# Four casts moved from ScalarE to VectorE, and a table load moved ahead of a copy, at the passage from attention to feed-forward

## The chip, the cores and the metric

The kernel runs on one core of one Trainium2 chip. The metric is the device time of one execution in microseconds (us). Engines are named as in the profile: PE is TensorE (matrix multiply; PEld are its weight loads, which overlap), ACT is ScalarE, DVE is VectorE, POOL is GpSimd, SP is SyncE, whose queue (SPq) issues nearly all transfers.

## The reference

One transformer layer on x of shape (4, 512, 512): cross-attention with 32 heads of 16 channels and rotary positions, added to x, and then a feed-forward part with ternary weights, added again. Cut to the parts that the change touches:

```python
x = x + xattn(layernorm(x), ctx, pos, ctx_pos, Wq, Wkv, Wout, bout)   # softmax attention
x = x + ffn(layernorm(x), w_fc, w_proj)

def ffn(x, w_fc, w_proj):
    h = bitlinear(x, w_fc)          # (4, 512, 512) -> (4, 512, 2048)
    h = gelu(h)                     # exact gelu
    return bitlinear(h, w_proj)     # back to 512

def bitlinear(x, w):                # x_hat is layernorm(x), rounded in the forward value
    return einsum('bsd,od->bso', x_hat, sign(round(w / mean|w|)) * mean|w|)
```

## The kernel before

**Attention.** For each of the 4 batches the 32 heads are taken in 8 groups of 4, so there are 32 groups, and each group has 8 units. A unit's logits are made twice: once with queries on the partitions (`logits`, for the row maxima, which VectorE reduces in `maxima`) and once with keys on the partitions, less the maxima (`exponentials`), of which ScalarE takes the exponential into a tile `es` (L570). Two such tiles are then multiplied with the values in `weigh` (L580), which gathers the group's `av` in one PSUM bank. `attended` ends a group: ScalarE copies `av` to the SBUF tile `avs` (L597), SP stores it (L598), and for every second group the sums are read back (L609), inverted on VectorE (L613), stored (L614), broadcast (L618) and multiplied into `aT` on GpSimd (L619). `aT` is the attended tile that the output projection reads.

**Passage.** The feed-forward part of batch 0 needs x of batch 0, normalised (`prepare`, L736, on VectorE), transposed on PE into PSUM (`first_T`, L749), and split into two parts: a high part `dTh` that is the value rounded to the matrix format fp32r (L753, a copy with a cast) and a low part `dTl`, the value less the high part (L754, VectorE). Four tiles of 128 tokens go through it. They are done during the last two groups of attention, as "chores" that `first_chore` puts into a queue. The chore's transposes come in one burst of units, the split is put off to the next one. All four tiles share one PSUM bank (`tp_d`), so the transposes of a tile wait for both readers of the tile before.

**Order.** The order on PE, DVE, ACT, SP and POOL is that in which the program text issues the work (a manual schedule). After the loop over bursts, the text weighs what is left, calls `attended` for the last group, runs everything that was put off (the split of the fourth tile among it), and then runs one gelu of a single column, so that the gelu table is loaded on ScalarE (L1006). A table load is an instruction of ScalarE's own queue.

**Feed-forward.** For each batch and each of 16 blocks of 128 hidden channels, `first` multiplies 8 times (L1039: four blocks of channels, high and low part) into a PSUM tile `hp` of which there are two, ScalarE takes gelu (L1047) into `h`; `split` makes the high part `hh` (L1053) and the square on ScalarE and the low part `hl` and the sums on VectorE; `second` multiplies them with the second matrix (L1077). The SBUF of the attention's tiles is given to the feed-forward's. The tiles of batches 1 to 3 go through the same `first_T`, but inside the feed-forward's loop, where `first_T(...)()` transposes and splits at once. At hidden blocks 6 to 9 of batch 0 the output projection of batch 3 is done (L1158).

Of the kernel before, what the change touches and what calls it, by code (L numbers as in the profile page):

```python
# [9 lines left out]
F32 = mybir.dt.float32  # L10
F32R = mybir.dt.float32r
AF = mybir.ActivationFunctionType
# [3 lines left out]
P = 128  # L16
# [15 lines left out]
def xattn_ffn(  # L32
# [13 lines left out]
    nc = tc.nc  # L46
# [5 lines left out]
    KD, KC, KF = D // P, C // P, F // P  # L52
# [18 lines left out]
    small = ctx.enter_context(tc.tile_pool(name="small", bufs=4))  # L71
# [84 lines left out]
    ones = const.tile([P, P], F32, name="ones")  # L156
# [136 lines left out]
    def put_off(k, f, end=0):  # L293
        later[end].setdefault(k, []).append(f)

    def run(k, end=0):
        for f in later[end].pop(k, []):
            f()

    def bank(name, spare=False):  # L300
        if spare:
            return ps_v.tile([P, S], F32, name=name, tag="v")
        if prologue[0]:
            return ps_s.tile([P, 2, S], F32, name=name, tag="s")[:, 0, :]
        return ps_t.tile([P, S], F32, name=name, tag="t")
# [267 lines left out]
    def weigh(i, c, es, av):  # L573

        b, g = divmod(i, NG)
        for r in range(2):
            for h in range(2):
                j = 2 * r + h
                v0 = (g * HG + j) * VS
                nc.tensor.matmul(  # L580
                    av[j * HP : (j + 1) * HP, :],
                    va[b % 2][:, c, v0 : v0 + HP],
                    es[r][:, h, :],
                    start=c == 0,
                    stop=c == NT - 1,
                )
# [3 lines left out]
    def attended(i, av, k):  # L590

        b, g = divmod(i, NG)
        n = g // 2
        avs = apool.tile([P, S], F32, name=f"avs{i}", tag="avs", bufs=1)
        nc.scalar.copy(avs, av)  # L597
        nc.sync.dma_start(av_d[b][g * P : (g + 1) * P, :], avs)  # L598
        if g == 0:
            aT[b] = big.tile([P, KD, S], F32, name=f"aT{b}", tag="aT", bufs=2)  # L600
        if g % 2 == 0:
            return
        rows = av_d[b][n * 2 * P : (n + 1) * 2 * P, :].rearrange("(h r) s -> h r s", r=HP)
        W = 2 * HG * S // P
        den = small.tile([P, W], F32, name=f"den{i}", tag="den", bufs=2)
        rec = rden_d[b][n * 2 * HG : (n + 1) * 2 * HG, :]

        def fetch():
            nc.sync.dma_start(den, rows[:, HD, :].rearrange("h (q w) -> h q w", w=W))  # L609
            nc.sync.dma_start(aT[b][:, n, :], rows[:, 0:HD, :])  # L610

        def invert():
            nc.vector.reciprocal(den, den)  # L613
            nc.sync.dma_start(rec.rearrange("h (q w) -> (h q) w", w=W), den)  # L614

        def spread():
            rb = big.tile([P, S], F32, name=f"rb{i}", tag="rb")
            nc.sync.dma_start(rb, rec.unsqueeze(1).to_broadcast([2 * HG, HD, S]))  # L618
            nc.gpsimd.tensor_tensor(aT[b][:, n, :], aT[b][:, n, :], rb, ALU.mult)  # L619

        put_off(k + 2, fetch, 1)
        put_off(k + 6, invert, 1)
        put_off(k + 7, spread, 1)
# [114 lines left out]
        )  # L738
        return d

    def first_T(i, d, tp):
        b, t = divmod(i, NT)
        if t == 0:
            dT[b] = (
                big.tile([P, KD, S], F32R, name=f"dTh{b}", tag="aT", bufs=2),
                big.tile([P, KD, S], F32R, name=f"dTl{b}", tag=f"va{b % 2}"),
            )
        for k in range(KD):
            nc.tensor.transpose(tp[:, k, :], d[:, k * P : (k + 1) * P], ident)  # L749

        def split():
            high, low = (x[:, :, t * P : (t + 1) * P] for x in dT[b])
            nc.scalar.copy(high, tp)  # L753
            nc.vector.tensor_tensor(low, tp, high.bitcast(F32), ALU.subtract)  # L754

        return split

    def first_chore(t, ready):
        split = []

        def step(p, _):
            split.append(first_T(t, first_d.pop(t), p.rearrange("p (k n) -> p k n", k=KD)))

        return Chore(f"tp_d{t}", 1, step, lambda p, k: put_off(k + 1, split[0]), 0.7, ready)

# [7 lines left out]
    p = bank("warm")  # L773
# [122 lines left out]
    av, es, first_d = {}, {}, {}  # L896
# [3 lines left out]
    for k, burst in enumerate(bursts):  # L900
        run(k)
        for kind, s in burst:
            i, u = divmod(s, NU)
# [48 lines left out]
        while due and due[0][0] <= k:  # L952
            _, j, c, e = due.pop(0)
# [43 lines left out]
    assert not queue and not urgent and open_chore is None, (len(queue), len(urgent))  # L997
    for _, j, c, e in due:
        weigh(j, c, e, av[j])
    left = sorted(later[0].keys() | later[1].keys())  # L1000
    attended(n_groups - 1, av.pop(n_groups - 1), left[-1])
    for k in left:
        run(k)
        run(k, 1)

    nc.scalar.activation(small.tile([P, 1], F32, name="gelu_1", tag="gelu_1"), ones[:, 0:1], AF.Gelu)  # L1006
    left = sorted(later[1])
    run(left[0], 1)
    order.__exit__(None, None, None)
# [21 lines left out]
    def xbank(name):  # L1031
        return ps_x.tile([P, KD, P], F32, name=name, tag="x")
# [96 lines left out]
    with tc.manual_schedule(engines=ordered):  # L1129
        gam4 = small.tile([P, NT], F32, name="gam4", tag="gam4")  # L1130
        nc.gpsimd.tensor_scalar(gam4, ones[:, 0:NT], gam_pr[:, 0:1], None, ALU.mult)
        steps = [(b, f) for b in range(B) for f in range(KF)]
        todo = list(steps)
        after = {}
        ds = {}
        hold = 0

        def behind(n, f):
            after.setdefault(n, []).append(f)


        for n, s in enumerate(left[1:]):
            behind(2 + n, lambda s=s: run(s, 1))

        for n in range(len(steps) + 4):
            on = n < len(steps)
            if on:
                b, f = steps[n]
                first(b, f)
                split(b, f)  # L1150
                if f == KF - 1 and b + 1 < B:
                    behind(n + 1, lambda b=b: totals(b))

            if on and b == 0 and 6 <= f < 6 + NT:
                t = f - 6
                p = xbank(f"op{B - 1}_{t}").rearrange("p k n -> p (k n)")
                for k in range(KD):
                    nc.tensor.matmul(  # L1158
                        p,
                        aT[B - 1][:, k, t * P : (t + 1) * P],  # L1160
                        wout_sb[:, k, :],
                        start=k == 0,
                        stop=k == KD - 1,
                    )
                i = (B - 1) * NT + t
                nc.vector.tensor_tensor(x_sb[:, i, :], p, x_sb[:, i, :], ALU.add)
            if on and b + 1 < B:
                at = (10, 11, 13, 14) if b == 0 else (6, 9, 12, 14)
                for t in range(NT):
                    i = (b + 1) * NT + t  # L1170
                    if f == at[t] - 4:
                        stats(i)
                    elif f == at[t] - 2:
                        ds[i] = prepare(i, fpool, "d")
                    elif f == at[t]:
                        first_T(i, ds.pop(i), xbank(f"tp_d{i}"))()
            if n == 3:
                nc.vector.tensor_copy(ones_r, ones)
            if n == 7:
                column_sums()  # L1180
            count = 0
            while todo and count < 2 and n >= hold:
                sb, sf = todo[0]
                m = sb * KF + sf
                if on and n - m < 2:
                    break
                if sb == B - 1 and sf >= KF - 2:
                    break
                todo.pop(0)
                count += 1  # L1190
                for t in range(NT):
                    second(sb, sf, t)
                if sf == KF - 1:
                    hold = n + 3
                    for t in range(NT):
                        behind(n, lambda b=sb, t=t: centered(b, t))
                        behind(n + 1 + t, lambda b=sb, t=t: finish(b, t))
                    break
            for x in after.pop(n, []):
                x()  # L1200
            if not on and len(todo) == 2:
                break
        for n in sorted(after):
            for x in after[n]:
                x()

        for t in range(NT):
            for sb, sf in todo:
                second(sb, sf, t)
            if t == 0:  # L1210
                totals(B - 1)
            centered(B - 1, t)
            if t > 0:
                finish(B - 1, t - 1)
        finish(B - 1, NT - 1)
# [50 lines left out]
```

## Time and profile before

| what | value |
|---|---|
| median of 3 runs | 845.94 us (845.82 to 846.93) |
| profiled execution | 843.32 us, span 841.5 us |
| PE busy | 813.5 us, 97% of the span |
| DVE busy | 616.3 us, 73% |
| ACT busy | 456.6 us, 54% |
| POOL busy | 299.9 us, 36% |
| clock granted to PE | 0.998 of full speed |
| cast of one tile on ACT (L753) | 16 of them, 578 ns in the mean |
| low part of one tile on DVE (L754) | 16 of them, 688 ns in the mean |
| table load on ACT (L1006) | 1283 ns |
| first matmul of the feed-forward | at 571.05 us |

The span is the time from the first to the last instruction that the profile shows; the execution's own time is a little longer. A row of the profile names the line of the program, the engine, the operation, what it writes and reads (tile names without their numbers), how often, and the busy time. A bracket such as `[1.07 <-DVE dTl L754]` says how long the engine was idle in front of the instruction, and which instruction ended that wait. In the rows of a stretch of time, the numbers are the length, then for each engine the busy time and the count of instructions, the clock granted to PE, the busy share of the 16 DMA engines and what they moved.

### The profile page before, as it was taken

To read this page: it belongs to the slowest core of one execution; us is meant where nothing else is said; L and a number is where in the kernel's file an instruction comes from. 1 tells how busy PE (TensorE), PEld (TensorE's weight loads), DVE (VectorE), ACT (ScalarE), POOL (GpSimd) and SP (SyncE) were. 2 spreads that over 40 slices of the span, in tenths; PEclk is the share of its full clock that TensorE was granted. 3 is DMA by queue.
4 is the path that set the end of the run, shared out by engine and by line. 5 is a ranking of instruction groups with operands and counts; after the bars stand their busy time and mean duration, and the time that the engine had idled before them with its cause. 6 is when DMAs were issued, how large, how long until landed. Compare 5 with 4: busy or idle time off the path is not lost. (4 is left out here: it accounts for less than half of the span.)

```text
span 841.5 us, 14323 instructions
## 1 busy us (share of the span) xinstructions
PE 813.5 (97%) x5572; PEld 434.7 (52%) x5572; DVE 616.3 (73%) x858; ACT 456.6 (54%) x604; POOL 299.9 (36%) x297
## 2 busy tenths in 40 slices
PE   7899999999999999999999999999999999999996
PEld 5234433344333334333334344337678888888885
DVE  7799778788878988787777867825465864964755
ACT  2347666575655546656555655576234544554442
POOL 3547265564923557576425721301000100100000
PEclk9999999999999999999999999999999999999999
DMA  7678596578695577959446657532000100100101
GB/s 232 172 263 279 199 308 218 187 259 269 207 322 166 167 261 252 315 174 298 168 151 210 231 178 278 174 111 94 1 0 1 51 1 0 51 1 1 51 0 51
DMA packets 75923, 133.65 MB, mean 159 GB/s; under 512 B 12240, under 2 KB 13776, under 8 KB 75344
## 3 DMA queue, kind: packets, MB, share of 16 engines
q1 hardware_dynamic: 74928, 132.08, 46.7%
q8 instruction: 44, 0.72, 0.4%
q10 hardware_dynamic: 928, 0.66, 0.3%
q14 instruction: 23, 0.19, 0.1%
HBM read 77.73 MB, written 53.94 MB: 156 GB/s over the span
## 5 line engine op out<-in xcount | busy, mean ns | idle before, releaser
L533 DVE TENSOR_REDUCE mx<-lp 128x2 f32<-128x1024 f32 x256 | 305.0, 1216 | 83.2 <-PE lp L519 82.8
L570 ACT ACTIVATE es<-sp 128x1024 f32<-128x1024 f32 x256 | 254.6, 1025 | 148.1 <-PE sp L566 139.6
L580 PE MATMUL av<-es,va 128*32 128x512 f32 x1024 | 136.0, 604 | 0.0
L558 PE MATMUL sp<-q_st,k_st 64*128 64x512 f32 x512 | 114.9, 445 | 8.0 <-DVE mx L533 7.1
L519 PE MATMUL lp<-k_st,q_st 64*128 64x512 f32 x512 | 111.6, 433 | 4.0 <-DMA q_st<-sl_q 2.1
L1047 ACT ACTIVATE h<-hp,gam_fc 128x512 f32<-128x512 f32 x64 | 44.1, 690 | 125.6 <-PE hp L1039 125.6
L1077 PE MATMUL fp<-wproj,hh 128*128 128x512 f32 x256 | 102.2, 399 | 0.0
L566 PE MATMUL sp<-mrows,sel 64*128 64x512 f32 x512 | 101.4, 392 | 0.2 <-ACT mrows L549 0.2
L1039 PE MATMUL hp<-dTh,wfc 128*128 128x512 f32 x256 | 100.0, 391 | 1.2 <-ACT dTh L753 1.2
L1039 PE MATMUL hp<-dTl,wfc 128*128 128x512 f32 x256 | 99.8, 390 | 0.2 <-DVE dTl L754 0.2
L1077 PE MATMUL fp<-wproj,hl 128*128 128x512 f32 x256 | 99.7, 390 | 0.0
L558 PEld LDWEIGHTS sp<-q_st,k_st 64*128 64x128 f32 x512 | 48.0, 184 | 82.9 <-DVE mx L533 43.6
L1066 DVE TENSOR_TENSOR acc<-acc,h 128x512 f32<-128x512 f32 x56 | 38.7, 691 | 70.2 <-ACT h L1047 70.2
L519 PEld LDWEIGHTS lp<-k_st,q_st 64*128 64x128 f32 x512 | 48.0, 184 | 74.0 <-ACT es L570 40.1
L619 POOL TENSOR_TENSOR aT<-aT,rb 128x512 f32<-128x512 f32 x16 | 21.2, 1325 | 132.7 <-DMA rb<-rden_d 129.6
L342 PE MATMUL qpq<-xT,wq_sb 128*32 128x512 f32 x512 | 62.9, 594 | 0.0
L1039 PEld LDWEIGHTS hp<-dTh,wfc 128*128 128x128 f32 x256 | 48.1, 188 | 12.0 <-ACT dTh L753 2.1
L1077 PEld LDWEIGHTS fp<-wproj,hh 128*128 128x128 f32 x256 | 48.1, 188 | 10.4 <-issue 0.7
L1039 PEld LDWEIGHTS hp<-dTl,wfc 128*128 128x128 f32 x256 | 48.1, 188 | 10.4 <-DVE dTl L754 0.5
L1077 PEld LDWEIGHTS fp<-wproj,hl 128*128 128x128 f32 x256 | 48.1, 188 | 10.3 <-issue 0.7
L566 PEld LDWEIGHTS sp<-mrows,sel 64*128 64x128 f32 x512 | 48.2, 185 | 5.8 <-ACT mrows L549 0.8
L222 POOL TENSOR_SCALAR r_a<-mv 128x1 f32<-128x1 f32 x16 | 4.7, 292 | 128.9 <-DVE mv L729 128.9
(148 smaller groups left out, 1058.8 us busy)
## 6 DMA issues: line engine op xcount, KB each, us to landing
k_st<-k_d SPq DMA_DIRECT2D x31, 512.0 KB
q_st<-q_d SPq DMA_DIRECT2D x31, 512.0 KB
av_d<-avs SPq DMA_DIRECT2D x32, 256.0 KB
k_d<-sh_k SPq DMA_DIRECT2D x30, 256.0 KB
k_d<-sl_k SPq DMA_DIRECT2D x30, 256.0 KB
q_d<-sh_q SPq DMA_DIRECT2D x30, 256.0 KB
q_d<-sl_q SPq DMA_DIRECT2D x30, 256.0 KB
wm<-in_wfcT SPq DMA_DIRECT2D x16, 256.0 KB
```

What stands on the lines that cost most here:

```text
L342: nc.tensor.matmul(p[j * HP : (j + 1) * HP, :], w[:, j * HP : (j + 1) * HP], x, start=start, stop=stop,)
L519: nc.tensor.matmul(lp[:, h, :], q_st[i][rows, r, t * P : (t + 1) * P], k_st[i][rows, r, :], start=True, stop=True,)
L533: nc.vector.tensor_reduce(mx[i][:, t, :, r], lp, AX.X, ALU.max, negate=True)
L558: nc.tensor.matmul(sp[:, h, :], k_st[i][rows, r, c * P : (c + 1) * P], q_st[i][rows, r, :], start=True, stop=False,)
L566: nc.tensor.matmul(sp[:, h, :], sel[rows, r, :], mrows[i][rows, :], start=False, stop=True)
L570: nc.scalar.activation(es, sp, AF.Exp, scale=1.0 / math.sqrt(HD))
L580: nc.tensor.matmul(av[j * HP : (j + 1) * HP, :], va[b % 2][:, c, v0 : v0 + HP], es[r][:, h, :], start=c == 0, stop=c == NT - 1,)
L619: nc.gpsimd.tensor_tensor(aT[b][:, n, :], aT[b][:, n, :], rb, ALU.mult)
L1039: nc.tensor.matmul(hp, wfc_sb[k][:, f * P : (f + 1) * P], dT[b][half][:, k, :], start=half == 0 and k == 0, stop=half == 1 and k == KD - 1,)
L1047: nc.scalar.activation(hid[b, f], hp, AF.Gelu, scale=gam_fc[:, 0:1])
L1066: nc.vector.tensor_tensor(acc[b][0], old, x, ALU.add)
L1077: nc.tensor.matmul(outs[b][t], parts[b, f][half][:, t * P : (t + 1) * P], wproj_sb[f], start=half == 0 and f == 0, stop=half == 1 and f == ...
```

## The change

The engine that casts the high part becomes an argument of `first_T`. The four tiles of batch 0, in `first_chore`, are cast with `nc.vector.tensor_copy`; the twelve tiles of batches 1 to 3, in the feed-forward's loop, still with `nc.scalar.copy`. So four casts leave ScalarE's queue and stand in VectorE's, each directly in front of the low part of the same tile. The gelu of one column, and with it the table load, moves from behind the last group's `attended` and everything that was put off to in front of it: on ScalarE it now stands between the last exponential and the last copy of `av`. Nothing else changes its order.

```diff
-    def first_T(i, d, tp):
+    def first_T(i, d, tp, e):
...
         def split():
             high, low = (x[:, :, t * P : (t + 1) * P] for x in dT[b])
-            nc.scalar.copy(high, tp)
+            e(high, tp)
             nc.vector.tensor_tensor(low, tp, high.bitcast(F32), ALU.subtract)
...
         def step(p, _):
-            split.append(first_T(t, first_d.pop(t), p.rearrange("p (k n) -> p k n", k=KD)))
+            tp = p.rearrange("p (k n) -> p k n", k=KD)
+            split.append(first_T(t, first_d.pop(t), tp, nc.vector.tensor_copy))
...
     for _, j, c, e in due:
         weigh(j, c, e, av[j])
+
+    nc.scalar.activation(small.tile([P, 1], F32, name="gelu_1", tag="gelu_1"), ones[:, 0:1], AF.Gelu)
     left = sorted(later[0].keys() | later[1].keys())
     attended(n_groups - 1, av.pop(n_groups - 1), left[-1])
     for k in left:
         run(k)
         run(k, 1)
-
-    nc.scalar.activation(small.tile([P, 1], F32, name="gelu_1", tag="gelu_1"), ones[:, 0:1], AF.Gelu)
     left = sorted(later[1])
...
                     elif f == at[t]:
-                        first_T(i, ds.pop(i), xbank(f"tp_d{i}"))()
+                        first_T(i, ds.pop(i), xbank(f"tp_d{i}"), nc.scalar.copy)()
```

## The prediction

> **What bounds the kernel now.** I read the page first (busy shares and slices), then the busy time of each engine around the passage (the table by stretches), then the instructions in order of time, engine by engine, then the groups with their shapes, and last the stretches of 0.2 us for the transfers. Every time without another name is in us from the span's start.
>
> The page, then the table by stretches (columns: length, busy time and count of PE, weight load, VectorE, ScalarE, GpSimd, clock, DMA share, GB/s):
>
> ```profile
> PE 813.5 (97%) x5572; PEld 434.7 (52%) x5572; DVE 616.3 (73%) x858; ACT 456.6 (54%) x604; POOL 299.9 (36%) x297
> ...
> 549.00:558.00 9.00, 8.78 (x62) 3.42 (x60) 1.65 (x5) 6.40 (x8) 0.00 (x0) 1.00 0.40 125
> 558.00:571.05 13.05, 10.38 (x75) 3.66 (x72) 2.09 (x4) 10.04 (x15) 0.00 (x0) 1.00 0.37 118
> 571.05:590.00 18.95, 18.72 (x81) 15.30 (x82) 12.94 (x19) 12.26 (x20) 2.97 (x2) 1.00 0.18 59
> ```
>
> TensorE bounds the whole. Before 558 and after 571.05 it idles 0.2 us; in the 13.05 us between it idles 2.67. This is the passage: the last eight exponentials, the four transposed tiles, the last copy. TensorE, then ScalarE, then VectorE, in order of time (the bracket is the idle time in front and who ended it):
>
> ```profile
> 566.00 1.10 PE L580 MATMUL av<-es,va 128*32 128x512 f32 x8
> 568.16 0.66 PE L749 MATMUL tp_d<-ident,d 128*128 128x128 f32 x4 [1.07 <-DVE dTl L754]
> 568.75 1.06 PE L580 MATMUL av<-es,va 128*32 128x512 f32 x8
> 571.05 0.49 PE L1039 MATMUL hp<-dTh,wfc 128*128 128x512 f32 x1 [1.24 <-ACT dTh L753]
> 571.78 0.50 PE L1039 MATMUL hp<-dTl,wfc 128*128 128x512 f32 x1 [0.23 <-DVE dTl L754]
> ...
> 566.78 0.60 ACT L753 CAST dTh<-tp_d 128x512 fp32r<-128x512 f32 x1
> 567.25 1.07 ACT L570 ACTIVATE es<-sp 128x1024 f32<-128x1024 f32 x1
> 569.93 0.59 ACT L597 COPY avs<-av 128x512 f32<-128x512 f32 x1 [1.61 <-issue]
> 570.41 0.59 ACT L753 CAST dTh<-tp_d 128x512 fp32r<-128x512 f32 x1
> 571.02 1.28 ACT L1006 ACT_TABLE_LOAD   x1
> 572.31 0.20 ACT L1006 ACTIVATE gelu<-ones 128x1 f32<-128x1 f32 x1
> 573.75 0.69 ACT L1047 ACTIVATE h<-hp,gam_fc 128x512 f32<-128x512 f32 x1 [1.24 <-PE hp L1039]
> ...
> 567.42 0.69 DVE L754 TENSOR_TENSOR dTl<-tp_d,dTh 128x512 fp32r<-128x512 f32 x1 [3.55 <-ACT dTh L753]
> 571.03 0.69 DVE L754 TENSOR_TENSOR dTl<-tp_d,dTh 128x512 fp32r<-128x512 f32 x1 [2.92 <-ACT dTh L753]
> ```
>
> The third tile's transposes end at 565.41, but its cast stands behind three exponentials on ScalarE and starts at 566.78; its low part ends at 568.11, and only then may the fourth tile's transposes (same PSUM bank) start. The fourth is transposed by 568.82, but its cast stands behind the last attended copy, which waits for av (569.81): cast 570.41 to 571.00, low part to 571.72, and the feed-forward's matmuls run freely only from 571.78. VectorE meanwhile waits 3.55 and 2.92 us.
>
> **Part 1: four casts go from ScalarE to VectorE.** Each takes 0.57 to 0.60 on ScalarE. On VectorE no row shows a one-source cast out of PSUM:
>
> ```profile
> L754 DVE TENSOR_TENSOR dTl<-tp_d,dTh 128x512 fp32r<-128x512 f32 x16 | 11.0, 688 | 11.4 <-ACT dTh L753 11.4
> L641 DVE TENSOR_TENSOR x_sb<-op,x_sb 128x512 f32<-128x512 f32 x12 | 8.1, 678 | 4.5 <-PE op L342 4.4
> L453 DVE CAST sh_q<-rot_q 128x512 fp32r<-128x512 f32 x1 | 0.4, 428 | 0.0
> ```
>
> Ends: 0.43 (same cast, SBUF source) and 0.69 (same tile out of PSUM, two sources). I take 0.69: the PSUM read is common, and the reduction of 1024 elements out of PSUM, 1.216, runs at the same rate per element. Lags, from the same rows: TensorE's end to VectorE's start 0.11 (556.86 to 556.97), VectorE or ScalarE to TensorE 0.05 to 0.06, VectorE to itself 0.03.
>
> - Tiles 1 and 2. TensorE in front of them waited for ScalarE's exponentials and the copy of the group before (562.65), not for the casts: ScalarE itself idles 0.47 and 0.91 right behind these casts, for av. Nothing is gained; VectorE does cast and low part at 557.52 to 558.93 (behind the d of L736) and 560.84 to 562.25, before each next transposes (560.07, 564.75).
> - Tile 3. Cast 565.52 to 566.21, low part 566.24 to 566.93. The transposes of tile 4 follow the av block of 566.00 directly, at 567.03 (a block is followed after 0.99 to 1.03, as at 559.08 to 560.07). Gain 568.16 - 567.03 = 1.13.
> - The last exponential no longer stands behind a cast: 566.80 to 567.85. The last av block starts 0.59 behind the transposes, at 567.62, and needs that exponential for its second half (568.15): no wait. It ends at 568.68.
> - Tile 4. Transposed by 567.69; cast 567.80 to 568.49; the first matmul of the feed-forward follows av at 568.61, 1.58 behind the transposes where it was 2.89: gain 1.31. Low part 568.52 to 569.21, second matmul 569.27, 0.66 behind the first where it was 0.73: gain 0.07.
>
> Sum 1.13 + 1.31 + 0.07 = 2.51 (2.77 with casts of 0.43). Behind VectorE's waiting casts stand the low parts, which needed the same tiles anyway, and the reciprocal of L613 with the transfers of L614 and L618 on SP. They come earlier too; the scaled aT is ready 3.5 us (587.9 to 591.4) ahead of its user L1158. The rest of VectorE's queue keeps its order, GpSimd does nothing from 549 to 571 (the table), and the order on TensorE is unchanged.
>
> **Part 2: gelu's table ahead of the last copy.** ScalarE is free at 567.85: load 1.28, gelu's first activation 0.20, so to 569.36. The copy was ready at 568.80 (av plus 0.12) and starts at 569.37, 0.57 later than it could. It issues the last store of av at 569.98. Nobody on TensorE waits for the copy, but the first gelu does for the store: in the built program h's memory lies over avs, so L1047's first instruction waits for that store to land, in both kernels. How long it takes:
>
> ```profile
> 570.54 0.33 SPq L598 DMA_DIRECT2D av_d<-avs  x1
> ...
> 571.20:571.40 0.20, 0.20 (x1) 0.04 (x1) 0.20 (x1) 0.20 (x1) 0.00 (x0) 1.00 0.19 72
> 572.00:572.20 0.20, 0.20 (x2) 0.16 (x2) 0.00 (x0) 0.20 (x1) 0.00 (x0) 1.00 0.33 113
> 572.20:572.40 0.20, 0.20 (x3) 0.16 (x2) 0.00 (x0) 0.19 (x2) 0.00 (x0) 1.00 0.00 0
> 573.00:573.20 0.20, 0.20 (x2) 0.16 (x2) 0.00 (x0) 0.00 (x0) 0.00 (x0) 1.00 0.06 8
> ```
>
> The store's bytes end shortly after 572.0. The small store behind it ends its bytes just after 573.0 and frees L618 at 573.49, 0.4 to 0.5 later. So the store lands about 572.5, 2.0 behind its issue, and was hidden: gelu started at 573.75 for hp. Now it lands about 572.0. Gelu, ready at 573.75 - 2.51 = 571.24, starts at about 572.07 and ends at 572.76. The third hp block, which reuses the first one's bank, could start at 575.32 - 2.51 = 572.81: it starts there, but its weights are not loaded ahead, which costs the first pair 0.34 instead of 0.23, so 0.11. With casts of 0.43 TensorE runs into the same gelu, so the end is the same. The first low part of h (0.69, from 573.45) is still 0.6 ahead of its matmul.
>
> The Trainium skill, "ScalarE: Activation LUTs", section "What ACT_TABLE_LOAD costs", gives a switch 1283 ns plus a drain of 1380, 2.66 in all. Here the load starts 0.02 behind the cast and the next activation 0.01 behind the load, so I charge 1.28; by the page's total the gain would be about 1.0.
>
> **Sum.** 2.51 - 0.11 = 2.40. The profiled execution: span 841.5 and 1.82 around it, 843.32; after: span 839.1, 840.9. It lies 2.62 below the median of the runs, 845.94. From 571 on TensorE is 97 to 99% busy and each stall of it is its own order's, so all 2.40 reaches the end: 845.94 - 2.40 = 843.5.
>
> **Rivals.**
> 1. *The gain is eaten by the store (no measurable change).* Each us that the store takes beyond 2.0 holds gelu, and through the bank TensorE, by one. At 2.8 to 4.4 the gain is 1.6 to 0: 844.3 to 845.9. For it: the wait is in the program, and the weight loads on the same queue, issued at 565.87, still move bytes at 570.6. Against: they end before this store starts moving, and the store before it also moved its bytes within 1.7 of issue.
> 2. *Slower, by the same wait.* It decides from a landing at 4.4 on; slower by 1.7 needs 6.1, which gives 847.6. Only the two 512 KB loads, 4.7 to their last bytes, come near, at twice the size.
> 3. *A table load holds ScalarE for twice its row*, another 1.28: copy at 570.65, store landed 573.29, gelu 573.35, bank free 574.09 instead of 572.81: gain 1.1, 844.8. Against: the 0.01 above. The page is the one named there.
> 4. *Larger gain*: the store lands 0.3 sooner and the cast takes 0.43: gain 2.77 at most, 843.2.
>
> **How the numbers follow.** Forecast 0.65; rival 1 0.13; rival 3 0.03; rival 4 0.13; rival 2 and every slower end 0.06. A measurement of this kernel tells about 0.2%, 1.7 us, from no change. Forecast and rival 4, with the upper edge of rival 1, make faster 0.80; the rest of rival 1 and rival 3 make same 0.15; slower 0.05. The range takes gains from 0.6 to 3.4: 2.77 and the 0.6 that the runs spread below (half of 845.82 to 846.93), and on the other side most of rival 1: 842.5 to 845.3.
>
> **What would show it.** Four casts of 0.43 to 0.69 on VectorE; no idle time in front of the fourth transposes, and 0.3 or less in front of each hp matmul; first hp near 568.6, second near 569.3; load at 567.9 directly behind the last exponential; last copy at 569.4; first gelu idle until about 572.1, ended by the store and not by hp. Wrong would be: a wait at the third hp block of over 0.3 (store or load longer), or an op matmul that waits for aT.

## The result, and the profile after

The changed kernel takes 843.01 us in the median (842.28 to 845.39) against 846.25 of the kernel before (845.82 to 846.93), in five executions of each: a ratio of 0.9969, with a 95% interval of 0.9957 to 0.9981, so 1.6 to 3.6 us less. The forecast was 2.40 us less and 843.5 us, counted from the 845.94 of the first three executions.

The two spans differ by less, 841.0 against 841.5 us, and that needs a word first. In the profiled execution of the changed kernel the passage begins 1.81 us later than in that of the kernel before: the first tile's transposes start at 558.01 instead of 556.20. The instructions up to there are the same on every engine. What differs in two places is the clock. Stretches around 14 and 276 us, of the kernel before and then of the changed one (the value behind the fifth engine is the granted clock):

```profile
14.00:20.00 6.00, 5.45 (x48) 2.74 (x52) 5.03 (x16) 2.67 (x5) 0.00 (x0) 1.00 0.44 161
276.00:282.00 6.00, 5.62 (x42) 2.16 (x46) 5.97 (x9) 2.86 (x3) 0.00 (x0) 1.00 0.53 165
```

```profile
14.00:20.00 6.00, 5.44 (x36) 3.91 (x40) 4.21 (x13) 2.35 (x4) 0.00 (x0) 0.72 0.49 182
276.00:282.00 6.00, 5.17 (x28) 1.78 (x30) 5.01 (x8) 2.05 (x2) 0.00 (x0) 0.72 0.45 138
```

In each of the two, TensorE ran at half speed for about 3.4 us (a mean of 0.72 over 6 us). The exponentials' starts, row by row in the two traces, lie 1.4 us apart behind the first dip, between 0.7 and 2.1 on the way and 1.8 at the passage; how much of the 1.8 the two dips make is not shown. So the passage is compared by its own length: **from the start of tile 1's transposes to the second matmul of the third hp block**, 575.54 - 556.20 = 19.35 us before and 574.95 - 558.01 = 16.93 now (from unrounded starts, as all lengths below). That is 2.41 less. Behind it both executions take 266.0 us to the end, and 266.1.

The page of the changed kernel, and its stretch that answers to 558.00 to 571.05 before, 1.81 later:

```profile
PE 815.7 (97%) x5572; PEld 435.8 (52%) x5572; DVE 619.6 (74%) x862; ACT 455.1 (54%) x600; POOL 300.2 (36%) x297
...
559.80:572.86 13.06, 12.69 (x85) 5.56 (x82) 5.22 (x9) 9.44 (x12) 0.00 (x0) 1.00 0.38 130
```

TensorE idles 0.37 us in it where it idled 2.67. The instructions of TensorE, ScalarE, VectorE and SP in order of time, the changed kernel:

```profile
568.84 0.66 PE L749 MATMUL tp_d<-ident,d 128*128 128x128 f32 x4
569.42 1.32 PE L580 MATMUL av<-es,va 128*32 128x512 f32 x8
570.67 0.50 PE L1040 MATMUL hp<-dTh,wfc 128*128 128x512 f32 x1
571.01 0.49 PE L1040 MATMUL hp<-dTl,wfc 128*128 128x512 f32 x1
...
574.61 0.50 PE L1040 MATMUL hp<-dTh,wfc 128*128 128x512 f32 x1
574.95 0.40 PE L1040 MATMUL hp<-dTl,wfc 128*128 128x512 f32 x1
```

```profile
565.86 3.77 ACT L570 ACTIVATE es<-sp 128x1024 f32<-128x1024 f32 x4 [1.40 <-PE av L580]
569.65 1.28 ACT L1002 ACT_TABLE_LOAD   x1
570.95 0.20 ACT L1002 ACTIVATE gelu<-ones 128x1 f32<-128x1 f32 x1
571.05 0.57 ACT L597 COPY avs<-av 128x512 f32<-128x512 f32 x1
573.87 0.69 ACT L1048 ACTIVATE h<-hp,gam_fc 128x512 f32<-128x512 f32 x1 [2.24 <-DMA rden_d<-den]
```

```profile
567.25 0.69 DVE L753 CAST dTh<-tp_d 128x512 fp32r<-128x512 f32 x1 [3.26 <-PE tp_d L749]
567.98 0.69 DVE L754 TENSOR_TENSOR dTl<-tp_d,dTh 128x512 fp32r<-128x512 f32 x1
569.53 0.69 DVE L753 CAST dTh<-tp_d 128x512 fp32r<-128x512 f32 x1 [0.86 <-PE tp_d L749]
570.25 0.69 DVE L754 TENSOR_TENSOR dTl<-tp_d,dTh 128x512 fp32r<-128x512 f32 x1
...
571.65 0.33 SPq L598 DMA_DIRECT2D av_d<-avs  x1
```

The waits of 1.07 and 1.24 us in front of the fourth transposes and the first hp matmul are gone. The exponentials run four in a row. The casts take 0.69 on VectorE. In their place stands one new wait, on ScalarE: the first gelu idles 2.24 us and starts 2.22 behind the issue of the last av store. The profile names the small store of the sums (`rden_d`), which lands at about the same time; experiment 4 shows that it is not that one.

### The profile page after: what moved, and what is told of

It reads as the page before. It is cut to its first block, busy times and chain, and to the rows that moved or that the text cites. A ratio compares the mean times of both kernels' runs of the same rounds, so it can differ in the third digit from the quotient of the medians.

```text
span 841.0 us, 14322 instructions
## 1 busy us (share of the span) xinstructions
PE 815.7 (97%) x5572; PEld 435.8 (52%) x5572; DVE 619.6 (74%) x862; ACT 455.1 (54%) x600; POOL 300.2 (36%) x297
## 4 chain that ended last, share of the span: by engine, by line
PE 81%; DVE 14%; issue 2%; ACT 1%; POOL 0%; DMA 0%; ACTq 0%; DVEq 0%; POOLq 0%
PE hp L1040 14%; PE fp L1078 14%; PE av L580 13%; PE sp L558 8%; DVE mx L533 7%; PE lp L519 7%; PE sp L566 5%; PE op L342 4%; PE qpq L342 4%; PE vp L342 3%; PE kpk L342 3%; PE op L1159 2%; PE mtp L545 1%; PE xtp L372 1%; DVE mparts L537 1%
```

## The experiments

All passages are in us, measured as above. Before: 19.35. Changed: 16.93.

### 1. The casts alone

```diff
     # casts as in the changed kernel; the table load back behind everything put off
-    nc.scalar.activation(small.tile([P, 1], ..., name="gelu_1", ...), ones[:, 0:1], AF.Gelu)
     left = sorted(later[0].keys() | later[1].keys())
     attended(n_groups - 1, av.pop(n_groups - 1), left[-1])
...
+    nc.scalar.activation(small.tile([P, 1], ..., name="gelu_1", ...), ones[:, 0:1], AF.Gelu)
     left = sorted(later[1])
```

> The four casts on VectorE, the table load in its old place behind the last copy. The measure is the passage: from the start of tile 1's transposes (L749) to the second matmul of the third hp block; it is 19.34 us in the kernel before and about 16.94 in the changed one. Theory (the casts alone make the gain, the moved load costs 0.57 on the copy and through the store 0.11 on TensorE): passage 16.83, the copy starts 0.1 behind the last av block, gelu's first instruction waits at most 0.3 for the store; time 2.5 us below before, not to be told from the changed kernel. Rival (the load behind the copy would have held the first gelu, so the move carries part of the gain): passage 17.3 or more, first gelu held by the load.

Measured: passage 16.76, ratio to the kernel before 0.9968 (0.9952 to 0.9985). Its profiled execution had no stretch at half clock up to the passage's end, as that of the kernel before had none, and so its span can be compared directly: 838.9 against 841.5, 2.6 less. ScalarE in it:

```profile
568.99 0.59 ACT L597 COPY avs<-av 128x512 f32<-128x512 f32 x1 [1.20 <-issue]
569.60 1.28 ACT L1007 ACT_TABLE_LOAD   x1
570.89 0.20 ACT L1007 ACTIVATE gelu<-ones 128x1 f32<-128x1 f32 x1
571.85 0.69 ACT L1048 ACTIVATE h<-hp,gam_fc 128x512 f32<-128x512 f32 x1 [0.76 <-DMA rden_d<-den]
```

The casts make the whole gain, and the moved load takes 0.17 of it away: even behind the copy, the load with its activation ends at 571.09, as the first hp block does (571.05). The first gelu waited 0.80 behind that block, not the 0.3 expected: the last av block ended 0.25 later than reckoned, and with it the copy and the store, and gelu started 2.24 behind the store's issue where the prediction had 2.09.

### 2. The moved load alone

```diff
     for _, j, c, e in due:
         weigh(j, c, e, av[j])
+    nc.scalar.activation(small.tile([P, 1], ..., name="gelu_1", ...), ones[:, 0:1], AF.Gelu)
...
-    nc.scalar.activation(small.tile([P, 1], ..., name="gelu_1", ...), ones[:, 0:1], AF.Gelu)
```

> The casts on ScalarE as before, only the table load moved ahead of the last copy. Theory: the load falls into ScalarE's idle time between the last exponential and the copy, which starts at the same point; passage 19.34, no change of the time (within 0.5 us). Rival (the move carries part of the gain): passage 18.8 or less, time 0.5 us or more below before.

Measured: passage 19.36, ratio 0.9999 (0.9984 to 1.0013). TensorE's rows are those of the kernel before, waits included:

```profile
572.28 0.66 PE L749 MATMUL tp_d<-ident,d 128*128 128x128 f32 x4 [1.07 <-DVE dTl L754]
572.87 1.06 PE L580 MATMUL av<-es,va 128*32 128x512 f32 x8
575.17 0.49 PE L1039 MATMUL hp<-dTh,wfc 128*128 128x512 f32 x1 [1.24 <-ACT dTh L753]
575.89 0.50 PE L1039 MATMUL hp<-dTl,wfc 128*128 128x512 f32 x1 [0.23 <-DVE dTl L754]
```

The move is worth nothing by itself; the rival that gave it part of the gain falls.

### 3. The last copy delayed by two more table loads

```diff
     nc.scalar.activation(small.tile(..., name="gelu_1", tag="gelu_1"), ones[:, 0:1], AF.Gelu)
+    nc.scalar.activation(small.tile(..., name="exp_2", tag="gelu_1"), ones[:, 0:1], AF.Exp)
+    nc.scalar.activation(small.tile(..., name="gelu_2", tag="gelu_1"), ones[:, 0:1], AF.Gelu)
```

> The changed kernel with two more table loads (exp, then gelu again, each with its one-column activation, 1.49 us each) ahead of the last copy, so the copy and its store come 2.97 us later. Theory (the first gelu waits for the store to land, and the third hp block for that gelu): passage 16.94 + 2.97 = 19.91, gelu's first instruction about 2.2 us behind the store's issue; time 0.6 us above before. Rival (the store does not hold gelu, only ScalarE's own queue does): copy to 572.9 on the clock of before, gelu right behind it, passage about 17.8.

Measured: passage 19.95, 3.02 longer than the changed kernel's, and a ratio to the kernel before of 0.9996 (0.9983 to 1.0010): the gain is gone. ScalarE, then the third hp block on TensorE:

```profile
570.47 1.28 ACT L1002 ACT_TABLE_LOAD   x1
571.76 0.20 ACT L1002 ACTIVATE gelu<-ones 128x1 f32<-128x1 f32 x1
571.97 1.28 ACT L1003 ACT_TABLE_LOAD   x1
573.26 0.20 ACT L1003 ACTIVATE exp<-ones 128x1 f32<-128x1 f32 x1
573.47 1.28 ACT L1004 ACT_TABLE_LOAD   x1
574.76 0.20 ACT L1004 ACTIVATE gelu<-ones 128x1 f32<-128x1 f32 x1
574.88 0.57 ACT L597 COPY avs<-av 128x512 f32<-128x512 f32 x1
577.71 0.69 ACT L1050 ACTIVATE h<-hp,gam_fc 128x512 f32<-128x512 f32 x1 [2.26 <-DMA rden_d<-den]
...
578.45 0.50 PE L1042 MATMUL hp<-dTh,wfc 128*128 128x512 f32 x1 [2.95 <-ACT h L1050]
```

The copy comes 3.0 later, the store is issued at 575.47, gelu follows 2.24 behind it, and TensorE waits 2.95 for gelu's bank. The price of one us for each us, which the first two rivals of the prediction were built on, is shown for this one delay (experiment 5 tells the store's part from ScalarE's own). The rows also settle the third rival: three loads follow each other with 1.50 from start to start, 1.28 of the load and 0.20 of the activation. The Trainium skill, "ScalarE: Activation LUTs", section "What ACT_TABLE_LOAD costs", puts 2.66 us on a switch, with a drain of 1.38; these rows have no room for the drain, and the measurement decides.

### 4. The last copy in memory of its own

```diff
-        avs = apool.tile([P, S], F32, name=f"avs{i}", tag="avs", bufs=1)
+        if i == n_groups - 1:
+            avs = big.tile([P, S], F32, name=f"avs{i}", tag="rb")
+        else:
+            avs = apool.tile([P, S], F32, name=f"avs{i}", tag="avs", bufs=1)
```

> The changed kernel with the last group's copy in memory that no tile of the feed-forward takes over (the slot of rb), so that no gelu waits for its store. Theory: gelu's first instruction starts 0.1 behind the first hp block, 0.8 us earlier than in the changed kernel, the third hp block is not held: passage 16.83; time as the changed kernel's, within noise. Rival (gelu is held by something else, such as the small store of the sums behind it): gelu still starts about 1 us behind the first hp block.

Measured: passage 16.75, ratio 0.9960 (0.9945 to 0.9974). ScalarE in it:

```profile
572.24 0.57 ACT L600 COPY avs<-av 128x512 f32<-128x512 f32 x1
574.17 0.69 ACT L1051 ACTIVATE h<-hp,gam_fc 128x512 f32<-128x512 f32 x1 [1.36 <-issue]
```

Gelu now starts 0.09 behind the first hp block, 0.9 earlier than in the changed kernel, though the small store of the sums is where it was. So the new wait was for the last av store alone, by the overlap of the two tiles in memory. It cost TensorE 0.18.

### 5. Both: late copy, own memory

```diff
     # the two loads of experiment 3 and the tile of experiment 4
```

> The two additional table loads of e3 and the copy's own memory of e4 together. Theory: the store no longer holds gelu, only ScalarE's queue does: gelu follows the late copy at once, passage about 17.8, 2.1 shorter than with the two loads alone. Rival (not the store but ScalarE's own delay made the loss of e3): passage as in e3, 19.9.

Measured, in a single execution, so without a ratio of times: passage 17.59. ScalarE, then the third hp block on TensorE:

```profile
572.52 0.57 ACT L600 COPY avs<-av 128x512 f32<-128x512 f32 x1
572.98 0.69 ACT L1053 ACTIVATE h<-hp,gam_fc 128x512 f32<-128x512 f32 x1
...
573.73 0.50 PE L1045 MATMUL hp<-dTh,wfc 128*128 128x512 f32 x1 [0.57 <-ACT h L1053]
```

ScalarE goes from the late copy to gelu without a wait, and TensorE waits 0.57 at the third hp block instead of 2.95. Of the 3.02 that the late copy cost, 2.36 were the store and 0.66 ScalarE's own queue (against 16.93).

### 6. Each cast done twice

```diff
             e(high, tp)
+            if e == nc.vector.tensor_copy:
+                e(high, tp)
```

> The changed kernel with each of the four casts done twice on VectorE, 0.72 more for each. Theory: tiles 1 and 2 have slack and cost nothing, tile 3 delays the next transposes by 0.67, tile 4 the first matmuls by 0.72, sum 1.39 at the second matmul; the store then no longer holds gelu, which gives 0.11 back: passage 16.94 + 1.28 = 18.22, time 1.3 us above the changed kernel. Rival (VectorE's casts are hidden): passage within 0.2 of 16.94.

Measured: passage 18.15, ratio 0.9988 (0.9966 to 1.0009). TensorE:

```profile
570.02 0.63 PE L749 MATMUL tp_d<-ident,d 128*128 128x128 f32 x4 [0.63 <-DVE dTl L756]
...
572.25 0.47 PE L1042 MATMUL hp<-dTh,wfc 128*128 128x512 f32 x1 [0.60 <-DVE dTh L755]
572.88 0.51 PE L1042 MATMUL hp<-dTl,wfc 128*128 128x512 f32 x1 [0.16 <-DVE dTl L756]
```

1.21 longer than the changed kernel's passage where 1.28 was expected, in the two places named, and none in front of the transposes of tiles 2 and 3. The casts of tiles 3 and 4 lie at the edge of the path on VectorE; in the changed kernel they just fit.

### 7, 8 and 9. Which tiles count

```diff
     # 7: tp, nc.vector.tensor_copy if t >= 2 else nc.scalar.copy     (the load moved)
     # 8: tp, nc.vector.tensor_copy if t == 2 else nc.scalar.copy     (the load in its old place)
     # 9: tp, nc.vector.tensor_copy if t == 3 else nc.scalar.copy     (the load moved)
```

> Only the casts of tiles 3 and 4 on VectorE, those of tiles 1 and 2 on ScalarE as before. Theory (the first two casts were never on the path): passage 16.94, as the changed kernel. Rival (relief of ScalarE counts for each cast): passage 17.5 or more.

> Only the cast of tile 3 on VectorE, the table load in its old place. Theory: the wait in front of the fourth transposes (1.07) goes and with it the delay of the last exponential, but the fourth cast still stands behind the last copy: passage 19.34 - 1.12 = 18.22, time 1.1 us below before. Rival (all of the gain comes from tile 4's cast getting past the copy): passage 19.3.

> Only the cast of tile 4 on VectorE, the table load ahead of the copy. The complement of the run with tile 3 alone, whose passage was 18.43 against 19.35 before. Theory (the two waits lie one behind the other and add up): the fourth transposes still wait for the third cast on ScalarE (1.07), the first hp block no longer stands behind the copy; second matmul of it about 1.4 earlier, passage 17.97. Rival (with tile 3 late, tile 4 brings nothing, because the last exponential or the copy sets the start anyway): passage 19.0 or more.

Measured: passages 16.95, 18.43 and 17.90 (7 and 9 in a single execution each, without a ratio of times). Tiles 1 and 2 add nothing, tile 3 alone gives 0.92, tile 4 alone 1.44, and the two sum to 2.36 of the 2.41. TensorE with tile 3 alone and then with tile 4 alone:

```profile
568.76 0.66 PE L749 MATMUL tp_d<-ident,d 128*128 128x128 f32 x4
569.35 1.31 PE L580 MATMUL av<-es,va 128*32 128x512 f32 x8
571.88 0.50 PE L1040 MATMUL hp<-dTh,wfc 128*128 128x512 f32 x1 [1.22 <-ACT dTh L753]
```

```profile
571.82 0.66 PE L749 MATMUL tp_d<-ident,d 128*128 128x128 f32 x4 [1.07 <-DVE dTl L754]
572.41 1.06 PE L580 MATMUL av<-es,va 128*32 128x512 f32 x8
573.41 0.49 PE L1040 MATMUL hp<-dTh,wfc 128*128 128x512 f32 x1
573.99 0.50 PE L1040 MATMUL hp<-dTl,wfc 128*128 128x512 f32 x1
```

Each keeps the wait that its missing cast makes. Tile 3 gave 0.2 less than reckoned, because the last av block becomes longer by 0.25 (1.31 instead of 1.06) once it starts early. In time, tile 3 alone has a ratio of 0.9984 (0.9967 to 1.0001), not told apart from no change by its interval; its 0.92 is read from the trace.

## Why the prediction was right

**The place and the sum.** 2.41 measured in the passage, 2.40 forecast. The place was right; that the sums agree to 0.01 is luck, since 0.07 more was gained than forecast up to the first hp block and 0.06 more was lost to the store. The step in front of the fourth transposes came out as forecast: 11.97 behind the start of tile 1 before, 10.83 now, a gain of 1.14 against 1.13. That the first two casts are worth nothing, and the moved load nothing or less, also held (experiments 7 and 2). Nor did the other sign of being wrong show, an op matmul that waits for aT: the profile of the changed kernel lists no wait of TensorE between 573 and 840, and from the passage to the end the two executions differ by 0.1 us.

**Two terms were off and cancelled.** The first hp matmul gained 1.06, not 1.31, and the second 0.39 more, not 0.07 (it is 0.34 behind the first, where 0.73 was and 0.66 was expected). The step that failed is "needs that exponential for its second half: no wait". The weight loads and the matmuls of the last av block before, then the last exponential and the block now:

```profile
568.75 0.16 PEld L580 LDWEIGHTS av<-es,va 128*32 128x32 f32 x8 [0.17 <-issue]
568.75 1.06 PE L580 MATMUL av<-es,va 128*32 128x512 f32 x8
```

```profile
568.59 1.04 ACT L570 ACTIVATE es<-sp 128x1024 f32<-128x1024 f32 x1
569.42 0.41 PEld L580 LDWEIGHTS av<-es,va 128*32 128x32 f32 x8 [0.17 <-issue]
569.42 1.32 PE L580 MATMUL av<-es,va 128*32 128x512 f32 x8
```

The block does not work through its two exponentials one behind the other. The first matmuls of its four 32-column groups start within 0.03 us of each other when all inputs are there; in the changed kernel, by the trace's single records, two start at 569.42 and two at 569.69, when the last exponential has just ended (569.63), and the block takes 1.32 instead of 1.06. This delay of 0.26 let the last low part be ready (570.94) before its matmul (571.01), so its own wait went. The sum at the second matmul is 2.58, against 2.51. That the two errors, 0.25 too much and 0.32 too little, nearly cancel is no accident: the second matmul needs the low part, and VectorE's chain to it does not pass through the av block. Experiment 9 shows it. There the exponential is in time, and the first hp matmul starts 1.58 behind the fourth transposes, as forecast, and the second 2.17, the same 2.17 as in the changed kernel. The 0.07 more come from the start of the fourth cast, 0.03 behind the transposes' end (569.53 against 568.84 + 0.66) where 0.11 was reckoned.

**The store.** Forecast: gelu starts 2.09 behind the store's issue, and TensorE loses 0.11, because the weights of the third hp block are not loaded ahead. Measured: gelu 2.22 behind the issue, TensorE loses 0.17 to 0.18 (2.58 less 2.41; experiment 4). Of this, the first pair of the block took 0.34 instead of 0.23, the 0.11 that was forecast; the other 0.06 is the later start of the block, behind the later gelu. The mechanism, worked out from the overlap in memory and not from any wait in the trace of before, was right, and the size small, because the third hp block wanted its bank at almost the moment at which gelu gave it back. Rival 1 needed 2.8 us or more from the store; it did not take that long.

**The casts' price.** 0.69, the upper of the two ends; out of PSUM the cast runs as slowly as the two-source subtraction. The Trainium skill, "VectorE: DVE Perf Modes", section "Why PSUM operands drop a tier", says that fp32 out of PSUM runs at single speed; 0.69 here against 0.43 for the same cast out of SBUF agrees.

**The rest of the time.** The median moved by 3.2 us, more than the passage. The interval (1.6 to 3.6) holds 2.4, and the one pair of profiled executions without clock dips, the kernel before and experiment 1, differs by 2.6 in span and by 2.58 in the passage. What of the 3.2 lies beyond is put down to the spread of the runs; that was not shown separately.

## What to carry to other kernels

Where a short step of a late stage stands in an engine's queue behind work that waits for the bound engine, look for an engine that idles there: the cast was slower on VectorE (0.69 against 0.59) and still gained 2.4 us, because of what it no longer stood behind. A wait that is hidden today, such as that for a store out of memory which the next stage takes over, has to be looked up in the program before work is pulled ahead; here about 1.0 us was left (gelu at 573.75, the store issued at 570.54, and the 2.2 us measured from issue to gelu), and the gain used it up. And compare a stage by its own length from a fixed instruction, since the executions of one kernel here differ by more than the effect (842.28 to 845.39 us).

## What the runs showed of the hardware

- The granted clock fell to half for about 3.4 us at a time, from 14.65 and from 277.48 us on, in the profiled execution of the changed kernel, in stretches whose instructions were the same as before. The Trainium skill, "TensorE: Matmul & The Clock Gate", section "Part 1: The HAM clock gate", ties half clock to an idle window of about 3.4 us, free-running. The first dip agrees: TensorE worked for 0.23 us in the 3.41 us in front of it. The second agrees less: it worked for 1.74. And the kernel before had as little work in stretches that answer to these (0.42 us between 11.00 and 14.60 in both kernels; 1.65 between 274.00 and 277.50, where the changed kernel had 1.83) and no dip, so little work alone does not bring one; what decides is not shown here.
- What a dip costs later on is not shown either: with two dips the changed kernel came to the passage 1.8 us later than the kernel before, experiment 5 with one (at 276.05) 0.3 later, and experiment 7 with one (at 15.54) 3.2. The five timed runs of the changed kernel spread from 842.28 us at a mean clock of 0.996 to 845.39 at 0.990.
- Matmuls onto different 32-column groups run side by side: the first four of a block start within 0.03 us and take 0.62 each. A block of eight took 1.06 us with all inputs there, and 1.32 with one of its two exponentials 0.26 late.
- A gelu that waited for a transfer started 2.2 us behind the issue of a 256 KB store in each of the kernels where it was held (2.22 in the changed kernel, 2.23 to 2.24 in experiments 1, 3, 7 and 9).
